# ConvNeXt block and two Mamba layers on one core: convolution bands read from DRAM in sliding runs, other group sizes, and a dt projection on three row groups

## The chip, the core and the metric

The kernel runs on one core of a Trainium2 chip. Times are microseconds of the device, from one launch of the whole program. The core has a matrix engine (PE, TensorE), a vector engine (DVE), an activation engine (ACT), a third engine for elementwise work and set-up (POOL, GpSimd), and SP, which here only issues transfers (DMA). Each engine works through its own list of instructions in order; a wait of one instruction holds all that stand behind it on that engine. SBUF is the on-chip memory with 128 partitions, PSUM the memory into which PE writes (8 banks of 128 x 512 floats), DRAM the memory outside.

## The reference

Input x is 32 x 96 x 56 x 56, float32. A ConvNeXt block comes first, then a Mamba block with two layers over the 3136 positions of each image, a fusion and a batch norm.

```python
# layer 0
h = depthwise_conv_7x7(x, conv_w, padding=3) + conv_b
h = layernorm over channels
h = gelu(h @ w1 + b1) @ w2 + b2          # 96 -> 384 -> 96
x1 = h * layer_scale + x
# layer 1, seq = x1 as (batch, 3136, 96)
for i in range(2):
    h = layernorm(seq); xs, z = split(h @ in_w)           # 192 each
    xc = silu(causal_conv4(xs) + conv_b)
    dt, Bm, Cm = split(xc @ xproj_w)                      # 6, 16, 16
    delta = softplus(dt @ dt_w + dt_b)                    # 192
    state = exp(delta * A) * state + delta * Bm * xc      # 192 x 16, a scan over positions
    seq = seq + ((state * Cm).sum + D * xc) * silu(z) @ out_w
out = fus_w @ concat(seq, relu(gp_w @ mean(x1))) + fus_b
out = batchnorm(out) + x1                                 # statistics over batch and positions
```

## The kernel before

**Groups of batches.** The depthwise convolution is done for two channels at a time (a pair; 48 pairs) as matmuls: the stationary operand is a band matrix that holds the seven vertical taps of one horizontal offset, the moving operand is the input with rows on partitions (112 = 2 x 56), batches and columns along the free dimension. Seven matmuls, one for each horizontal offset dw, add up in one PSUM bank. The batches come in groups (lines 101 to 103): the first has 12, then four of NB = 5. The output goes to DRAM (`conv_d`), 56 rows for each channel.

**Head.** `conv_pair` (line 158) does the first group for each pair: load x, write the seven vertical taps into three rotating band tiles with seven predicated copies on DVE (L165, masks made by POOL), store the band in DRAM (`band_d`), two halves of six batches with seven matmuls each (L176), an activation that adds the bias (L180), and the store (L184). Set-up of the weights stands between the third and the fourth pair in the program: POOL loads them, small matmuls (L270, L294, L301) fold norm and output weights. Then batch 0 goes through the rest of the ConvNeXt block.

**Loop.** 4 chunks of 784 positions for each of 32 images and 2 layers make 256 stages. A stage has 24 scans (slots), j = 0 to 5 for 32 channels each and g = 0 to 3 for four of the 16 states each. For each, ACT computes the exp (L904, after a copy of the carried state L903), DVE the product with B (`times_b`, L886) and the scan (L958), POOL the product with C (L963) and, for j = 2 and 5, that with B (`pooled`, L940); PE spreads u over the states (L930) and sums the result (L1004, `add_up`). Two exps and the spread values pass through the wide PSUM tiles. `gate` (L979) multiplies with silu(z).

All other work is put between the scans by an order written by hand. `put(m, pieces)` files each piece under a slot number of stage m (a fraction orders pieces in one slot), and the main loop emits, slot by slot, exps, `keep_state`, the scan, spreads, `add_up` and then the pieces. The numbers fix the order within each engine's list, not the time. Pieces of the stage are:

- `prep` of the next stage: norm, projections (L624), `dbl` and `dbl_out` (xproj, 38 output rows, L651 and L659), `dt` (L686: six matmuls of 6 rows by 64 columns, all from partitions 0 to 5), `softplus` (L694, three), `product` u = delta * xc on POOL (L706), and the loads that spread delta, B and C over partitions (`load_d4`, three buffers; `load_bc`; `store_u` and `load_u`).
- `post` of the stage before: output projection (`project`, L785 and L791) and `move` (L799 or L805), statistics.
- `block0`, the ConvNeXt block for half a chunk of a later image: centre (L371), squares (L376), norm, L443, gelu, L463, residual (L469).
- `conv`, one pair of a later group (192 of them, from stage 2 on): loads of band and x (`load`), seven matmuls (`tap`, L555), activation and store (`store`, L564, L567). All seven write PSUM bank set 2, which the third softplus has to release.

`keep_warm` (L916) issues spare matmuls into an unused part of a PSUM bank; `FILL` says how many go ahead of a spread. `KS` says how many scans after its own a state is kept, `AHEAD` where `pooled` stands.

**Tail.** Batch statistics, then for each half image two loads, an activation (L1108), an addition (L1109) and a store.

## Time and profile before

| | us |
|---|---|
| median of 3 runs | 15847.34 (15838.45 to 15850.79) |
| profiled execution, its time | 15850.69 |
| its span, first to last instruction | 15848.7 |
| first convolution on PE (L176) | 47.7 to about 446 |
| first to last scan (L958) | 565.3 to 15474.8 |

| instruction | mean ns | count |
|---|---|---|
| scan L958 | 1771 and 1776 | 6144 |
| product with B on DVE, L886 | 980 and 967 | 4096 |
| product with C on POOL, L963 | 3251 | 3072 |
| exp on ACT, L904 | 918 and 947 | 6144 |
| predicated copy L165 | 1038 | 336 |

A line of the profile names engine, source line, operation and tiles (out<-in). A matmul of float32 stands in the trace as two passes, each with a weight load of its own. "Idle before" is the time in which an engine stood still just before an instruction, with what released it. Busy time of instructions that follow each other directly overlaps a little, so that distances between starts are the better measure of pace.

### The profile page before, as it was taken

To read this page: it belongs to the slowest core of one execution; us is meant where nothing else is said; L and a number is where in the kernel's file an instruction comes from. 1 tells how busy PE (TensorE), PEld (TensorE's weight loads), DVE (VectorE), ACT (ScalarE), POOL (GpSimd) and SP (SyncE) were. 2 spreads that over 40 slices of the span, in tenths; PEclk is the share of its full clock that TensorE was granted. 3 is DMA by queue.
4 is the path that set the end of the run, shared out by engine and by line. 5 is a ranking of instruction groups with operands and counts; after the bars stand their busy time and mean duration, and the time that the engine had idled before them with its cause. 6 is when DMAs were issued, how large, how long until landed. Compare 5 with 4: busy or idle time off the path is not lost. (4 is left out here: it accounts for less than half of the span.)

```text
span 15848.7 us, 213573 instructions
## 1 busy us (share of the span) xinstructions
PE 13987.3 (88%) x74328; PEld 5953.8 (38%) x74328; DVE 15121.7 (95%) x11782; ACT 11958.4 (75%) x23139; POOL 14379.5 (91%) x4766
## 2 busy tenths in 40 slices
PE   8899999999999999999999999999998888888870
PEld 5333333333333333333333333333333333333320
DVE  8699999999999999999999999999999999999993
ACT  1587777778787787877777787877777777777763
POOL 1599999999999999999999999999999999999990
PEclk9899999999999999999999999999999999999985
DMA  4355545455545454545455455455444444444438
GB/s 111 110 149 150 154 148 153 148 150 153 152 148 153 148 151 151 152 148 152 149 150 154 147 153 149 150 151 152 148 151 136 140 142 137 137 138 143 138 126 293
DMA packets 1307217, 2362.54 MB, mean 149 GB/s; under 512 B 495918, under 2 KB 697914, under 8 KB 1306136
## 3 DMA queue, kind: packets, MB, share of 16 engines
q1 hardware_dynamic: 1296808, 2308.46, 48.1%
q10 hardware_dynamic: 7168, 38.54, 0.6%
q8 instruction: 585, 9.58, 0.2%
q14 instruction: 496, 4.06, 0.1%
q0 software_dynamic: 2160, 1.88, 0.1%
HBM read 1945.97 MB, written 402.41 MB: 148 GB/s over the span
## 5 line engine op out<-in xcount | busy, mean ns | idle before, releaser
L963 POOL TENSOR_TENSOR h<-h,cp 128x1568 f32<-128x1568 f32 x3072 | 9938.5, 3251 | 548.4 <-DVE h L958 467.0
L958 DVE TENSOR_TENSOR_SCAN h<-w,h 128x785 f32<-128x785 f32 (+1 forms) x3072 | 5299.7, 1771 | 117.2 <-ACT w L904 100.7
L958 DVE TENSOR_TENSOR_SCAN h<-da,w 128x785 f32<-128x785 f32 (+1 forms) x3072 | 5391.0, 1776 | 2.7 <-ACT da L904 2.7
L940 POOL TENSOR_TENSOR h<-us,bp 128x1570 f32<-128x1570 f32 x1024 | 3321.2, 3243 | 31.0 <-PE y L1004 19.3
L904 ACT ACTIVATE w<-d,A 128x784 f32<-128x784 f32 x3072 | 2819.0, 918 | 500.5 <-DVE h L958 419.0
L886 DVE TENSOR_TENSOR w<-w,bp 128x786 f32<-128x786 f32 x3072 | 2916.4, 980 | 200.1 <-PE w L930 85.4
L904 ACT ACTIVATE da<-d,A 128x784 f32<-128x784 f32 x3072 | 2876.7, 947 | 14.9 <-DMA d<-dd 14.1
L1004 PE MATMUL y<-h,ssum 128*32 128x392 f32 x24576 | 2590.9, 511 | 59.2 <-POOL h L963 59.2
L624 PE MATMUL ps<-hn,wx 97*64 97x392 f32 x12288 | 2202.8, 500 | 28.4 <-POOL hn L615 28.4
L930 PE MATMUL w<-u,sel 64*128 64x393 f32 x4096 | 986.4, 556 | 940.8 <-DVE h L958 929.3
L1004 PEld LDWEIGHTS y<-h,ssum 128*32 128x32 f32 x24576 | 691.0, 111 | 1710.8 <-issue 1356.4
L624 PEld LDWEIGHTS ps<-hn,wx 97*64 97x64 f32 x12288 | 812.2, 136 | 1353.2 <-issue 1285.3
L555 PE MATMUL ps<-xpad,band 112*112 112x280 f32 x2688 | 909.8, 458 | 284.0 <-ACT dl L694 284.0
L903 ACT COPY w<-st 128x1 f32<-128x1 f32 x2304 | 371.0, 161 | 1038.6 <-DVE h L958 1005.6
L916 PEld LDWEIGHTS y<-sel 128*128 128x128 f32 x7680 | 920.0, 192 | 251.2 <-DVE h L958 113.7
L886 DVE TENSOR_TENSOR h<-w,bp 128x786 f32<-128x786 f32 x1024 | 990.3, 967 | 0.5 <-DMA bp<-bd 0.5
L367 ACT ACT_TABLE_LOAD x759 | 973.8, 1283 | 14.2 <-PEq L1157 0.8
L916 PE MATMUL y<-sel 128*128 128x120 f32 x7680 | 967.5, 279 | 12.1 <-DVE z L979 12.1
L615 POOL TENSOR_TENSOR hn<-seq,hn 96x784 f32<-96x784 f32 x256 | 478.1, 1868 | 462.3 <-ACT hn L388 455.4
L791 PE MATMUL ps<-z,ow 64*96 64x392 f32 x3072 | 849.2, 706 | 0.0
L930 PEld LDWEIGHTS w<-u,sel 64*128 64x128 f32 x4096 | 329.5, 188 | 1328.2 <-DVE h L958 748.9
L555 PEld LDWEIGHTS ps<-xpad,band 112*112 112x112 f32 x2688 | 437.6, 186 | 868.0 <-ACT dl L694 402.6
(159 smaller groups left out, 16539.9 us busy)
## 6 DMA issues: line engine op xcount, KB each, us to landing
d<-dd SPq DMA_DIRECT2D x1536, 392.0 KB, 3.7
bp<-bd SPq DMA_DIRECT2D x1024, 392.0 KB, 5.5
cp<-bd SPq DMA_DIRECT2D x1024, 392.0 KB, 6.6
us<-uu SPq DMA_DIRECT2D x512, 392.0 KB, 5.0
dd<-dl SPq DMA_DIRECT2D x512, 294.0 KB, 3.8
band<-band_d SPq DMA_DIRECT2D x192, 343.0 KB, 7.8
uu<-u SPq DMA_DIRECT2D x1024, 49.0 KB, 2.6
cv<-conv_d SPq DMA_DIRECT2D x256, 147.0 KB, 2.7
```

The costliest lines, as they stand in the source:

```text
L367: nc.scalar.preload_act_table_set("natural_log_exp_and_others")
L555: nc.tensor.matmul(v["ps"][0:R2, 0 : NB * W], v["band"][:, dw, :], xpad[:, :, dw : dw + W], start=(dw == 0), stop=(dw == 6),)
L624: nc.tensor.matmul(v["x", q][rows(a), 0:HC], weights[:, k, 64 * q : 64 * q + 64], v["hn"][:, o : o + HC], start=(k == 0), stop=(k == last),)
L791: nc.tensor.matmul(v["ps"][a][0:C, 0:HC], S.d["ow"][rows(a), q, :], S.z[rows(a), q, :], start=False, stop=(q == NQ - 1),)
L886: nc.vector.tensor_tensor(halves(S.pb[j, g]), halves(S.u4[j])[:, :, 0 : HC + 1], halves(S.bc[0, g // 2][:, g % 2, :]), ALU.mult,)
L904: nc.scalar.activation(e[:, 1 : 1 + CH], S.d4[j], AF.Exp, scale=S.d["A"][:, j, g : g + 1])
L916: nc.tensor.matmul(spare, sel[:, 0, :], sel.rearrange("p a b -> p (a b)")[:, 0 : 512 - HC], start=True, stop=True,)
L930: nc.tensor.matmul(u4[:, 512 * a : 512 * a + HC + 1], sel[rows(a), j % 2, :], S.u[rows(a), j // 2, a : a + HC + 1], start=True, stop=True,)
L940: nc.gpsimd.tensor_tensor(states(S, j, h)[:, :, 0 : 1 + CH], S.us[j].unsqueeze(1).broadcast_to([128, 2, 1 + CH]), S.bc[0, h][:, :, 0 : 1 + ...
L958: nc.vector.tensor_tensor_scan(h[:, g % 2, at], S.e.pop((j, g))[:, at], S.pb.pop((j, g), h[:, g % 2, :])[:, at], 1.0 if c else 0.0, ALU.mu ...
L963: nc.gpsimd.tensor_tensor(h[:, :, 0:CH], h[:, :, 1 : 1 + CH], S.bc[1, g // 2], ALU.mult)
L1004: nc.tensor.matmul(S.y[r0 : r0 + 32, 0:HC], ssum, hs[k][:, g, tok(a)], start=False, stop=(half == 1 and g == 1),)
```

## The change

There are six parts.

1. Groups: 8 batches first, then four groups of 6.
2. Bands: one line of 1024 floats for each channel holds its taps at a pitch of 128, 14 copies of it are written to DRAM, and a band tile is loaded with two transfers in which each partition reads a run of 896 floats (3584 bytes) that starts one float earlier than that of the partition before. Masks, predicated copies and the store of bands go.
3. Output rows of a channel lie at a pitch of 64 in PSUM and in `conv_d`; 120 rows are computed and stored, eight of them unused.
4. xproj has 128 output rows; dt's six rows appear three times, at partitions 0, 32 and 64, B and C at 96 to 127. The tile shares the buffer of the gelu. The dt projection takes its three groups from these three places, the third first, and softplus follows that order.
5. FILL from 3 and 12 to 1 and 11, KS from 2 to 3, AHEAD exchanged for j = 2. `warm(0)` calls `keep_warm` with zero matmuls.
6. Slots of many pieces.

```diff
+HP = 64
+REP, PER = 14, 1024
-    NB = 5
+    NB = 6
-    groups = [(0, b0)] + [(b, b + NB) for b in range(b0, B, NB)]
+    groups = [(0, b0)] + [(b, min(b + NB, B)) for b in range(b0, B, NB)]
...
-    band_d = dram.tile([C // 2, 2 * H, 7 * 2 * H], F32, name="band_d")
+    band_d = dram.tile([C, REP * PER], F32, name="band_d")
...
+    cw = cc.tile([C, 49], F32, name="cw")
+    nc.sync.dma_start(cw, conv_w)
+    line = cc.tile([C, PER], F32, name="line")
+    nc.vector.memset(line, 0.0)
     for dh in range(7):
...
+        nc.vector.tensor_copy(
+            line.rearrange("p (k n) -> p k n", n=P2)[:, 0:7, HP + H + 2 - dh],
+            cw[:, 7 * dh : 7 * dh + 7],
         )
...
+    for lo in range(0, C, 24):
+        r = slice(lo, lo + 24)
+        nc.sync.dma_start(
+            band_d[r].rearrange("c (r n) -> c r n", n=PER),
+            line[r].unsqueeze(1).broadcast_to([24, REP, PER]),
         )
...
+    def load_band(T, p):
+        for j in range(2):
+            w = band_d[2 * p + j]
+            nc.sync.dma_start(
+                T[j * H : (j + 1) * H],
+                bass.AP(
+                    w.tensor, w.offset + HP + H - 1 - HP * j,
+                    [[PER - 8, H // 8], [PER - 1, 8], [1, 7 * P2]],
+                ),
+            )
...
-        for dh in range(7):
-            nc.vector.copy_predicated(
-                T,
-                masks[dh].unsqueeze(1).broadcast_to([R2, 7, R2]),
-                cw[:, p, dh * 7 : (dh + 1) * 7].unsqueeze(2).broadcast_to([R2, 7, R2]),
+        load_band(T, p)
+        ps = cps.tile([M2, b0 * W], F32, name="ps")
+        for dw in range(7):
+            nc.tensor.matmul(
+                ps, T[:, dw * P2 : dw * P2 + M2], xp[:, :, dw : dw + W],
+                start=(dw == 0), stop=(dw == 6),
             )
-        nc.sync.dma_start(band_d[p], T.rearrange("p k n -> p (k n)"))
...
+        ct = cx.tile([M2, b0 * W], F32, name="ct")
+        nc.scalar.activation(ct, ps, AF.Identity, bias=cb[0:M2, p : p + 1])
+        nc.sync.dma_start(conv_d[0][p * P2 : p * P2 + M2, :], ct)
...
+        d["xp"] = const.tile([128, NQ, 128], F32, name=f"xp{i}", tag=f"xp{i}")
+        nc.vector.memset(d["xp"], 0.0)
+        for q in range(NQ):
+            nc.vector.tensor_copy(d["xp"][:, :, 32 * q : 32 * q + DTR], xp[:, :, 0:DTR])
+        nc.vector.tensor_copy(d["xp"][:, :, 128 - 2 * NS :], xp[:, :, DTR:NX])
...
-                (-6, load), (2, load_x), (11.2, center), (11.9, square), (12.4, mean),
-                (12.6, root), ((14.1, norm) if ZP else (14.1, True, norm)), (15, up), (15.2, gelu), (17.3, down),
-                (17.7, residual),
+                (-6, load), (2, load_x), (11.2, center), (12.1, square), (12.4, mean),
+                (12.6, root), ((14.6, norm) if ZP else (14.6, True, norm)), (15, up), (15.2, gelu), (17.4, down),
+                (18.8, residual),
...
-            at = (5.7, 5.9, 8, 8.7, 9, 9.4, 10.2)
-            return [(-1, load), (10.3, store), *[(at[dw], tap(dw)) for dw in range(7)]]
+            at = (5.4, 6.5, 8, 8.7, 9, 9.4, 10.2)
+            return [(-0.5, load), (11.8, store), *[(at[dw], tap(dw)) for dw in range(7)]]
...
-        AHEAD = {(2, 0): 0.5, (2, 1): 4.4, (5, 0): 12.3, (5, 1): 16.9}
+        AHEAD = {(2, 0): 4.9, (2, 1): 0.8, (5, 0): 11.2, (5, 1): 16.9}
...
-                v["dbl"] = wp.tile([NX, CH], F32, name="dbl", tag="dbl", bufs=1)
+                t = wp.tile([128, NF, HC], F32, name="gl", tag="gl", bufs=1)
+                v["dbl"] = t.rearrange("p f n -> p (f n)")[:, 0:CH]
...
-                    for a in range(2):
+                for a in range(2):
+                    for q in (2, 0, 1):
+                        r = slice(32 * q, 32 * q + DTR)
                         nc.tensor.matmul(
-                            v["dt", q][rows(a), 0:HC], d["dtw"][:, 64 * q : 64 * q + 64],
-                            v["dbl"][0:DTR, tok(a)], start=True, stop=True,
+                            v["dt", q][rows(a), 0:HC], d["dtw"][r], v["dbl"][r, tok(a)],
+                            start=True, stop=True,
                         )
...
-                for q in range(NQ):
+                for q in (2, 0, 1):
                     nc.scalar.activation(
...
-                (-18, load), (-12.3, center), (-11.9, square), (-12.1, halo), (-11.6, mean),
-                (-11.2, root), (-9.5, norm),
+                (-18, load), (-12.2, center), (-11.9, square), (-17, halo), (-11.6, mean),
+                (-11.4, root), (-9.5, norm),
...
-            t = (-4.5, -4.4, -5.8, -4.8, -4.2, 0.2, 1.3, 2.3, 2.9, 3.4, 4)
+            t = (-4.5, -4.4, -5.8, -4.5, -4.2, -0.2, 1.3, 2.7, 2.9, 3.9, 5.1)
...
-                (max(10, t[8] + 1.2), load_bc(0, 0)), (max(10.2, t[8] + 1.2), load_bc(1, 0)),
-                (max(16.8, t[8] + 2.2), load_bc(1, 1)), (max(19.8, t[8] + 2.2), load_bc(0, 1)),
+                (max(10.1, t[8] + 1.2), load_bc(0, 0)), (max(10.2, t[8] + 1.2), load_bc(1, 0)),
+                (max(19.5, t[8] + 2.2), load_bc(1, 1)), (max(17.2, t[8] + 2.2), load_bc(0, 1)),
...
-                (max(14, t[10] + 1.5), product), (max(17.1, t[10] + 3.1), store_u(0)),
-                (29, store_u(1)),
-                (max(18.1, t[10] + 2), load_d4(0)), (max(21.9, t[10] + 3), load_d4(1)),
-                (max(20.3, t[10] + 3.2), load_u(0)), (24, load_d4(2)),
-                (26.9, load_d4(3)), (32.9, load_u(1)), (30, load_d4(4)), (34, load_d4(5)),
+                (max(16.7, t[10] + 1.5), product), (max(18.9, t[10] + 3.1), store_u(0)),
+                (27, store_u(1)),
+                (max(13.9, t[10] + 2), load_d4(0)), (max(21.9, t[10] + 3), load_d4(1)),
+                (max(22, t[10] + 3.2), load_u(0)), (24, load_d4(2)),
+                (27.1, load_d4(3)), (32.9, load_u(1)), (28.1, load_d4(4)), (30.2, load_d4(5)),
...
-            pieces = [(7.9, project), (8.9, move(0)), (9.2, move(1))]
+            pieces = [(7.5, project), (8.7, move(0)), (9.1, move(1))]
...
-                pieces += [(12.7, save), (17.2, stat(0)), (18.7, stat(1))]
+                pieces += [(12.7, save), (17.2, stat(0)), (20.9, stat(1))]
...
-        KS = 2
-        FILL = {0: 3, 4: 12}
+        KS = 3
+        FILL = {0: 1, 4: 11}
...
+            put(m, [(4.5, warm(0)), (12.5, warm(0))])
```

## The prediction

> **What bounds the kernel now.** First the page's busy times: four engines carry load, and VectorE (DVE) nearly all of the span.
>
> ```profile
> PE 13987.3 (88%) x74328; PEld 5953.8 (38%) x74328; DVE 15121.7 (95%) x11782; ACT 11958.4 (75%) x23139; POOL 14379.5 (91%) x4766
> ```
>
> A mean over stages hides where the rest is, so next the busy time by stretches (columns: stretch, length, then PE, weight loads, DVE, ACT, POOL, then granted PE clock, DMA share, GB/s): the first convolution, a piece of the scan loop with convolution in it, one without, and the last pass.
>
> ```profile
> 100.00:400.00 300.00, 300.00 (x1054) 184.00 (x1053) 273.54 (x264) 40.54 (x75) 0.00 (x0) 1.00 0.45 120
> 2700.00:4700.00 2000.00, 1846.42 (x9950) 785.93 (x9952) 1971.34 (x1522) 1592.66 (x3110) 1930.04 (x630) 0.95 0.50 151
> 13200.00:15200.00 2000.00, 1747.09 (x9368) 707.23 (x9362) 1954.10 (x1510) 1554.62 (x3031) 1915.40 (x625) 0.92 0.44 139
> 15440.00:15840.00 400.00, 27.53 (x144) 9.54 (x144) 153.19 (x105) 130.67 (x117) 36.65 (x12) 0.53 0.89 291
> ```
>
> Three regimes, then. The head (to the first scan, 565 us) is bound by PE: 300 of 300 us. The loop (256 stages of 24 scans, 565 to 15476, so 58.2 us each) is bound by DVE, 98.6% busy in one row and 97.7% in the other; the row with the lower clock is the one with less DVE work done. The tail (some 370 us of it) is bound by DMA, and the diff doesn't touch it.
>
> In the head the timeline gives the pace:
>
> ```profile
> 299.79 146.19 PE L176 MATMUL ps<-xpad,band 112*112 112x336 f32 x512
> 302.27 7.49 DVE L165 COPY_PREDICATED band<-mi,cw 112x784 f32<-112x784 int32 x7 [0.52 <-PE ps L176]
> 310.26 7.50 DVE L165 COPY_PREDICATED band<-mi,cw 112x784 f32<-112x784 int32 x7 [0.49 <-PE ps L176]
> ```
>
> 512 passes in 146.19 us are 0.2855 us each; a matmul is two passes, a pair of channels 14 matmuls, so 7.99 us, which is the distance of the two DVE rows (310.26 - 302.27). DVE needs 7.5 of it and waits for PE: PE sets the pace.
>
> In the loop the waits tell what could be won (waiter, line, releaser: total, times, longest):
>
> ```profile
> DVE h L958 <- ACT w L904: 100.7, 114, 2.6
> DVE w L886 <- PE w L930: 85.4, 83, 47.7
> ACT sq L564 <- PE ps L555: 327.1, 192, 2.9
> ACT seq L799 <- PE ps L791: 104.0, 74, 2.7
> ```
>
> DVE waits 100.7 us for exps and 37.7 for spreads (85.4 less the single wait of 47.7 before the loop runs), with small ones some 145 us. That is the ceiling of what reordering can win here. ACT's waits for PE precede them: ACT is in order, and an exp stands behind the activation that waits.
>
> **The change, head.** (1) Batches 12 to 8. A pair takes 7 matmuls of 8 x 56 = 448 columns instead of 14 of 336. In proportion to columns a pass is 0.2855 x 448/336 = 0.381 us, 14 passes 5.33 us. 48 pairs: 255.8 against 383.7, so -128 us. The output rows (120 for 112) don't lengthen a pass. ACT's copy, 0.54 us for 336 columns twice, is one of about 0.7: hidden under PE.
>
> (2) The band. The 336 predicated copies (1.04 us) and 21 selects go; one line per channel is made by 7 small copies and written 14 times to DRAM, 5.5 MB. At the 291 GB/s of the tail that is 19 us, behind the bias loads, whose issue took 2.1 and 10.2 us on SP; the first band can be in SBUF at some 45 to 50 us.
>
> (3) PE's order moves: the built program has all twelve set-up matmuls (norm weights, folded output weights) ahead of the first pair; before, one was ahead and the others lay between pairs.
>
> ```profile
> L301 PE MATMUL ps<-fw,owt x12: 246/297/422, 85.0 to 92.5; 96*64 96x96 f32 x12
> ```
>
> Their last ran at 92.5, but between convolution matmuls. Their inputs are POOL's small loads, issued until 70.6 us; the one that counts (ow of the second layer) was issued at 62.9-64.1 and takes 4.2 to land, then three rounds of some 1.5 us: about 73. The loads themselves meet 5.5 MB of band writes; POOL loses about 9 us of selects and clears. Bounds 65 and 90 us; I take 75, since the chain keeps its loads. So the convolution runs from 75 to 75 + 255.8 + 0.7 = 331.5 us instead of from 47.7 to 446.5: head -115 us (-125 to -100). Work after it (446.5 to 565) stays.
>
> (4) The pace needs the loads. A pair moved 952 KB in 7.99 us at 0.45 DMA share; now it moves 201 (x) + 401 (band) + 215 (store) = 817 KB in 5.33 us, which is 153 GB/s, share 0.58 by that row: hidden. [...] By the row the loads take 3.1 us of 5.33[...]
>
> **The change, loop.** (5) Convolution taps, 280 to 336 columns: by columns a pass goes from 0.238 (0.2855 x 280/336) to 0.2855 us, fourteen passes +0.67 us of PE in each of 192 stages. (6) The dt projection goes from one group of array rows to three, so that its six matmuls can stand side by side instead of two and two.
>
> ```profile
> 4078.76 2.56 PE L686 MATMUL ps<-dbl,dtw 6*64 6x392 f32 x12
> 4082.94 1.67 PE L555 MATMUL ps<-xpad,band 112*112 112x280 f32 x4 [1.62 <-ACT dl L694]
> 4084.40 2.74 PE L785 MATMUL ps<-seq,eye 96*96 96x392 f32 x4
> ```
>
> Before, 2.56 us for twelve passes in two column groups. Bounds: 2.56 (no gain) and two passes, 0.65; the nearest row is this pairing itself, so I take 1.2, -1.3 us. Three spare matmuls of 120 columns fewer per stage (FILL, 15 to 12; two passes of 0.10): -0.6. In sum PE has about 1.2 us less a stage; as PE doesn't bound, this pays only through what waits for it.
>
> (7) It does: the second row shows PE idle 1.62 us for the third softplus, which frees the bank of the taps. With group 2 first, tap 0 starts two activations (0.96 us) earlier; two longer taps cost 0.2 to 0.4 back, so the project behind (L785, L791), for which ACT's move waits, comes about 0.6 us earlier. A stall of that chain is 0.73 us long (DVE waits at 3511.9 for an exp that stood behind a move released at 3511.2). (8) The residual and the convolution's store go one exp later in ACT's queue, as do the squares. This removes stalls of the kind below, where DVE lost 2.59 us because the exp stood behind the residual:
>
> ```profile
> 12486.03 1.79 DVE L958 TENSOR_TENSOR_SCAN h<-w,h 128x785 f32<-128x785 f32 x1 [2.59 <-ACT w L904]
> 12484.32 0.58 ACT L469 ACTIVATE xin<-ps,b2ls 96x392 f32<-96x392 f32 x1 [2.85 <-PE ps L463]
> ```
>
> What is late next is the residual's own store, with a wait of half a stage before its reader. Between nothing and 145 us, I take 60 (four tenths; the chains of (7) and (8) are most of the 100.7, but not all of each goes).
>
> (9) Moves on SP and POOL. The product goes behind one more L963, yet POOL's row has the same sum, and its gap of 1.06 us a stage stays. On SP the fifth d4 load goes ahead of the store of delta and waits for an exp of scan 7: that store goes some 6 us later, about 15 us ahead of its reader. The sixth goes ahead of the u load of group 5 and waits for an exp of scan 11, at 4093.6; the u load then lands (median 5.0) near 4099, where POOL wanted it at 4099.2. The 1.06 us gap behind hides it; without it POOL, with only 1.6 us free in a stage, would be late. The keep_state and halo moves and warm(0), which issues nothing, cost nothing: 0.2 us copies beside ACT's 25% idle.
>
> [...] In the stage from 4069.4 PE's longest gap is 1.62 us, and yet the clock between 4083 and 4090 was 0.76. [...]by the row it may: kept as a rival.
>
> **Sum.** Against the profiled execution (span 15848.7, time 15850.69): head -115, loop -60, so 15675.7. The median of the runs is 3.35 below that execution: 15672, taken as 15670.
>
> **Rivals.** *Loop unchanged*: the DVE rows are 98% busy, and stalls can move instead of going. Then 15847 - 115 = 15732. *DMA bounds the pairs*: [...]against it the DMA share of 0.45. *All stalls go*: -115 - 140: 15592. *Slower*: PE's shorter dt and fewer fillers leave its clock halved for one more window of about 3.4 us in slots 4 to 9; PE is then 1.7 us late at the project, 0.6 of it already won, and DVE waits about 0.5 us in every stage. The row at clock 0.92 against 0.95 gives the sign: 17 us per 2000 us, 0.5 a stage. 256 x 0.5 = +128 against -115: 15860. It decides from 0.45 us a stage on, and ends slower from 0.57.
>
> **How the numbers follow.** Likeliest 0.50 (15620 to 15720 on its own), loop unchanged 0.20, DMA bound 0.12, all stalls gone 0.08, halved clock 0.10. A measurement tells 0.2%, 32 us, from no change. All but the last are faster; of the last half is slower, 0.04 the same. Range 15570 to 15790: it takes in the first four.
>
> **What would show it.** Right: L178 passes of some 0.38 us, pairs 5.3 us apart from 65-90 to about 330; the first scan near 450; L700's twelve passes in under 1.6 us; the exp waits of L972's scans under 60 us. Wrong: gaps of PE for band loads in the head; a granted clock under 0.93 in the loop with longer waits of the scan for exps; POOL waiting for us.

## The result

The changed kernel takes 15760.28 us (median of 4 runs, 15745.14 to 15764.96) against 15842.9 of the kernel before on the same chip: ratio 0.9946, 95% interval [0.9929, 0.9963]. That is 83 us less, 0.5%; 177 were forecast. The direction and the range were right, the size was off by a factor of two.

Where the time went, in the two profiled executions (first to last scan is the distance between the starts of the first and the last scan):

| stretch | before | after | difference | forecast |
|---|---|---|---|---|
| start to first scan | 565.3 | 466.4 | -98.9 | -115 |
| first to last scan | 14909.5 | 14924.0 | +14.5 | -60 |
| last scan to the end | 373.9 | 369.5 | -4.4 | 0 |
| span | 15848.7 | 15759.8 | -88.9 | -175 |

So the head gave most of what it should, and the loop gave nothing that can be told from noise (see the experiments). First the page's busy times of the changed kernel, then the stretches that answer to those of before (columns as there):

```profile
PE 13461.7 (85%) x72120; PEld 5646.6 (36%) x72120; DVE 14771.9 (94%) x11457; ACT 11966.7 (76%) x23091; POOL 14367.3 (91%) x4746
```

```profile
100.00:300.00 200.00, 200.00 (x528) 95.77 (x528) 0.00 (x0) 23.47 (x37) 0.00 (x0) 1.00 0.55 155
2600.00:4600.00 2000.00, 1798.16 (x9752) 762.75 (x9750) 1969.82 (x1523) 1596.21 (x3108) 1929.36 (x631) 0.95 0.51 153
13100.00:15100.00 2000.00, 1677.64 (x9182) 680.23 (x9174) 1952.53 (x1509) 1560.98 (x3030) 1914.56 (x624) 0.91 0.43 138
```

DVE's predicated copies in the head are gone (336 of 1.04 us), and it is idle there (0.00 of 200 us in the first row). In the loop it is as busy as before (1969.82 of 2000 against 1971.34), although PE is busy 48 us less in a stretch of the same length. Most of the gain sits in the first row: PE works without a gap. The timelines of the head give its pace, of PE and of ACT:

```profile
99.83 200.59 PE L178 MATMUL ps<-xpad,band 112*120 112x448 f32 x528
...
103.82 0.63 ACT L183 ACTIVATE ct<-ps,cb 120x448 f32<-120x448 f32 x1 [4.68 <-PE ps L178]
109.14 0.63 ACT L183 ACTIVATE ct<-ps,cb 120x448 f32<-120x448 f32 x1 [4.68 <-PE ps L178]
```

200.59 / 528 is 0.380 us a pass and 5.32 us lie between two pairs. In the loop the table of waits shows that those which were to go did shrink, and that one has grown, that of the gate (waiter, line, releaser: total, times, longest; the last line is the gate's of the kernel before):

```profile
DVE w L900 <- PE w L947: 93.8, 40, 49.1
DVE h L975 <- ACT w L918: 63.9, 80, 3.3
DVE z L996 <- PE y L1021: 63.9, 76, 6.1
...
ACT sq L575 <- PE ps L565: 159.4, 192, 2.5
...
ACT seq L813 <- PE ps L805: 54.0, 33, 2.7
...
DVE z L979 <- PE y L1004: 13.0, 5, 5.3
```

The scan's waits for an exp fell from 100.7 to 63.9 us, ACT's for the taps from 327.1 to 159.4, for the project from 104.0 to 54.0. Those for spreads, without the single one before the loop, rose from 37.7 to 44.7. Against that the gate (L996) now waits 63.9 us for the summed result; it was 13.0. By slots, over stages 4 to 249: DVE's waits before the scan of slot 10 fell from 54.7 to 21.8 us, those before the scan of slot 19 from 31.0 to nothing, and the gate, which stands between the scans of slots 19 and 20, got 46.5.

To compare loops I use one number per stage, its loss: the distances from the start of each scan to that of the next, less the undisturbed distance of the same slot (its 5th percentile), summed over the 24 slots. It is worked out from the starts of scans in the kept traces. Over the 184 stages 10 to 193, which have convolution taps, the mean is 0.62 us before and 0.64 after. The stalls moved; the sum stayed.

### The profile page after: what moved, and what is told of

Same layout as the page of the kernel before. It is cut to its first block, busy times and chain, and to the rows that moved or that the text cites. A ratio compares the mean times of both kernels' runs of the same rounds, so it can differ in the third digit from the quotient of the medians.

```text
span 15759.8 us, 207713 instructions
## 1 busy us (share of the span) xinstructions
PE 13461.7 (85%) x72120; PEld 5646.6 (36%) x72120; DVE 14771.9 (94%) x11457; ACT 11966.7 (76%) x23091; POOL 14367.3 (91%) x4746
## 5 line engine op out<-in xcount | busy, mean ns | idle before, releaser
L975 DVE TENSOR_TENSOR_SCAN h<-w,h 128x785 f32<-128x785 f32 (+1 forms) x3072 | 5287.1, 1769 | 73.0 <-ACT w L918 63.9
L565 PE MATMUL ps<-xpad,band 112*120 112x336 f32 x2688 | 1060.1, 512 | 331.4 <-ACT dl L708 331.4
L930 PEld LDWEIGHTS y<-sel 128*128 128x128 f32 x6144 | 747.1, 192 | 259.0 <-issue 97.0
L930 PE MATMUL y<-sel 128*128 128x120 f32 x6144 | 794.6, 279 | 21.1 <-DVE z L996 21.1
L384 ACT ACTIVATE sq<-ps 96x392 f32<-96x392 f32 x768 | 378.7, 493 | 557.6 <-PE ps L379 392.7
L565 PEld LDWEIGHTS ps<-xpad,band 112*120 112x120 f32 x2688 | 449.6, 191 | 935.2 <-ACT dl L708 446.5
```

The costliest lines, as they stand in the source:

```text
L565: nc.tensor.matmul(v["ps"][0:M2, 0 : nb * W], band[:, dw * P2 : dw * P2 + M2], xpad[:, 0:nb, dw : dw + W], start=(dw == 0), stop=(dw == 6),)
L930: nc.tensor.matmul(spare, sel[:, 0, :], sel.rearrange("p a b -> p (a b)")[:, 0 : 512 - HC], start=True, stop=True,)
L975: nc.vector.tensor_tensor_scan(h[:, g % 2, at], S.e.pop((j, g))[:, at], S.pb.pop((j, g), h[:, g % 2, :])[:, at], 1.0 if c else 0.0, ALU.mu ...
```

## The experiments

Medians are of 4 or 5 executions (21 for conv_only and softplus_order, 13 for after_taps280); ratios are to the kernel before (after: as above). "Loop" is first to last scan in the one profiled execution. Three executions with the very same loop code gave 14924.0, 14920.5 and 14912.8. A profiled execution can lie further off: that of fill_back took 16.5 us less than its kernel's median and that of loop_only 15.6 less, those of bias_row 14.5 and conv_dt 10.0 more. So a loop difference under some 15 us says nothing, and where these four stand in one the medians decide.

| run | what it is | median | ratio | first scan | loop |
|---|---|---|---|---|---|
| before | | 15841 to 15847 | 1 | 565.3 | 14909.5 |
| conv_only | before + convolution's part | 15822.7 | 0.9988 | 462.6 | 14988.4 |
| conv_dt | conv_only + dt, softplus order | 15797.5 | 0.9966 | 463.9 | 14962.7 |
| fill_back | the change with FILL of before | 15762.0 | 0.9945 | 467.3 | 14903.7 |
| after | the change | 15760.3 | 0.9946 | 466.4 | 14924.0 |
| taps280 | conv_only, shorter taps | 15738.4 | 0.9931 | 462.5 | 14902.5 |
| after_taps280 | the change, shorter taps | 15830.7 | 0.9992 | 468.5 | 14996.7 |
| loop_only | before + all but the convolution's part | 15931.6 | 1.0055 | 565.8 | 14980.4 |
| loop_fill | loop_only with FILL of before | 15914.1 | 1.0045 | 565.8 | 14981.2 |
| dt_before | before + dt, softplus order | 15925.2 | 1.0053 | 569.5 | 14982.3 |
| softplus_order | before + softplus order | 15858.8 | 1.0010 | 568.5 | 14921.9 |
| conv_dt_sq4 | conv_dt, four buffers for squares | 15763.8 | 0.9952 | 465.3 | 14923.8 |
| bias_row | the change, biases as one row | 15724.6 | 0.9926 | 439.2 | 14920.5 |

### What each part does to the loop

Four kernels stand between the two. The first takes only the convolution's part; the second adds the dt projection:

```diff
 # conv_only: the changed kernel, but
-            at = (5.4, 6.5, 8, 8.7, 9, 9.4, 10.2)
+            at = (5.7, 5.9, 8, 8.7, 9, 9.4, 10.2)
...
-        FILL = {0: 1, 4: 11}
+        FILL = {0: 3, 4: 12}
 # and all other slots, KS, AHEAD, xproj and dt as before
 # conv_dt: the same, but xproj, dt and the softplus order of the change
```

> The changed kernel with the loop's slots, FILL, KS, AHEAD, xproj and dt projection of the kernel before: only the groups, the sliding bands and the row pitch are new. Theory A (the loop's gain was given back by the matrix engine's clock, which fewer spare matmuls let fall): first scan near 466 us as in the changed kernel, first to last scan 14910 (+-10) as in the kernel before, so some 100 us faster than before in all (15745). Theory B (the larger taps, 336 columns for 280, cost the loop): first to last scan 14930 to 14960, and 40 to 80 us faster in all (15765 to 15800).

> As the run with the convolution's part alone, but with the dt projection on three row groups and the softplus order of the changed kernel; slots, FILL, KS and AHEAD as before. Theory A: the exps' waits in slot 10 fall by half (54.7 to some 25 us), first to last scan 14870 to 14900, time 15705 to 15735. Theory C (a stall removed from slot 10 comes back at the next meeting point, whatever the fillers): first to last scan within 10 us of the run with the convolution's part alone. The twelve passes of dt take 1.2 us or less against 2.56.

The convolution's part alone brings 18 us (ratio 0.9988 [0.9982, 0.9995]): 103 in the head, of which the loop takes 79 back. That was theory B, and more than the 20 to 50 us it allowed for the loop. The dt projection and softplus order take 26 off the loop and 25 off the time. That lies between the two theories of conv_dt: the waits of slot 10 did fall to 25 us as theory A had it, but the loop stayed far above its 14900. The slots with KS and AHEAD (from conv_dt to fill_back) take 36 off the time; the 59 between the two profiled loops are too large, since one execution was slower and the other faster than its median. FILL comes last:

```diff
 # fill_back: the changed kernel, but
-        FILL = {0: 1, 4: 11}
+        FILL = {0: 3, 4: 12}
```

> The changed kernel with 3 and 12 spare matmuls in place of 1 and 11. Theory A: the granted clock in slots 15 and 16 is full again (lost 0.44 us a stage now), the gate's waits for the summed result (L996 for L1021, 63.9 us) fall below 20, the loop is 30 to 60 us shorter: 15700 to 15730. Theory C: the gate's waits stay above 45 and the time is within 10 us of the changed kernel (15750 to 15770).

The clock in slots 15 and 16 came back to full and the gate's waits fell from 63.9 to 33.6 us, but the median is the same (15762.0 against 15760.3). Over the 184 stages the loss in slot 19 fell from 32 us to nothing, that in slots 12 to 14 rose from 21 to 53: a stall that moved. Theory A fell on it, since its lost clock was real and its return brought nothing; theory C's time (15750 to 15770) came true.

So in this order of steps a gain of the forecast size was there (25 and 36 us by the medians, in place of 60), but on a loop that the convolution's part had first made 79 us longer. The next run asks whether it is the length of the taps:

```diff
 # taps280: conv_only, but
-                        v["ps"][0:M2, 0 : nb * W], band[:, dw * P2 : dw * P2 + M2],
-                        xpad[:, 0:nb, dw : dw + W],
+                        v["ps"][0:M2, 0 : (5 if dw else nb) * W], band[:, dw * P2 : dw * P2 + M2],
+                        xpad[:, 0 : 5 if dw else nb, dw : dw + W],
```

> The run with the convolution's part alone, but in the loop only the first of the seven taps covers all six batches of a later group, the other six cover five (280 columns in place of 336): most of the convolution of the sixth batch of each later group is left out. Theory L (the 79 us that the convolution's part adds to the loop, 14988.4 us from first to last scan against 14909.5, come from the length of the taps): 14915 to 14930, time 15755 to 15775. Theory D (they come from the band in two transfers of runs, the stores with 120 rows, or the other row pitch): 14970 or more, time 15810 to 15830.

Theory L, and more than it asked (14915 to 14930): some 0.57 us less of PE's work a stage (by columns, twelve passes of 280 in place of 336) takes 86 us off the loop, and 84 off the time. Band loads in two transfers, stores of 120 rows and the pitch cost nothing that shows: the loop takes 14902.5 us with them and 14909.5 in the kernel before.

### The loop's part by itself

```diff
 # loop_only: the kernel before with dt, softplus order, slots, FILL, KS, AHEAD of the change
 # dt_before: the kernel before with dt and softplus order only
 # softplus_order: the kernel before, but
-                for q in range(NQ):
+                for q in (2, 0, 1):
```

> The kernel before with only the loop's part of the change that is not convolution: dt on three row groups, softplus order, slots, FILL, KS, AHEAD. Theory P (steps 6 to 8 were right in their place, and the convolution's longer taps took their gain): first to last scan 14830 to 14860 in place of 14909.5, time 15765 to 15795. Theory C (stalls removed come back at the next meeting point by themselves): 14890 or more, 15825 or more. With the taps short, the gate's waits for the summed result stay under 25 us by theory P, over 45 by theory C.

> The kernel before with only dt on three row groups and the softplus order. Theory P (steps 6 and 7 right in their place): the exps' waits of slot 10 (54.7 us) fall by half or more, first to last scan 14909.5 to 14870-14890, time 15800 to 15820. Theory C (a stall that goes comes back at the next meeting point): 14900 to 14920, 15830 to 15850. Theory K (1.3 us less of PE's work lets its clock fall and costs more than it brings): 14930 or more, 15860 or more.

> The run with the loop's part alone on the kernel before (15931.6), with 3 and 12 spare matmuls as before in place of 1 and 11. Theory A (fewer spare matmuls let PE's clock fall in slots 15 and 16, and the summed result comes late to the gate): clock lost there 0.53 us a stage to under 0.1, the gate's waits 72.5 us to under 25, first to last scan 14980.4 to 14930 or less, time 15885 or less. Theory C (the gate's waits go and others take their place): 14965 or more, 15915 or more.

> The kernel before with only the softplus order of the change (third group first). Theory P (step 7: tap 0 comes 0.96 us earlier, and so the project and its move): waits of slot 10 from 54.7 to 25-40 us, first to last scan 14880 to 14900. Theory K (what comes earlier before the spread of slot 10 widens the gap there, clock lost in slots 11 and 12 from 0.03 to 0.4-0.8 a stage): 14915 to 14950, time 15850 to 15885; the rest of the 73 us belongs to the shorter dt.

This was the surprise. On the kernel before, the loop's part makes it slower: ratio 1.0055 [1.0041, 1.0069]. The dt projection with its softplus order alone does the same, 1.0053 [1.0041, 1.0066]; putting the spare matmuls back in loop_fill leaves the profiled loop where it was (14981.2 against 14980.4) and the medians 17.5 us apart, with intervals that overlap (ratio 1.0045 against 1.0055), so their share is small at most. The softplus order alone costs 12 us of the loop and 15 of the time, with 0.65 us of lost clock a stage in slots 11 and 12, as theory K had it. So theory P fell. Theory C, for which stalls only come back, left loop_only open (14890 or more), but not dt_before (14900 to 14920). K was right in size: a dt projection that is 1.6 us shorter, with its softplus order, made the loop 73 us longer. (The edit also widens xproj to 128 rows and lets its result share the gelu's buffer. Neither shows in the trace: the copy of that result takes 476 ns in both kernels, and PE's weight loads wait 179 us for it in place of 197.) Each half of the change alone costs the loop 71 or 79 us, both together 14.5.

The trace of dt_before shows how. Its PE around slot 10 (start, duration; idle before in brackets):

```profile
4106.97 0.97 PE L697 MATMUL ps<-gl,dtw 6*64 6x392 f32 x12
...
4118.74 1.21 PE L563 MATMUL ps<-xpad,band 112*112 112x280 f32 x4
4122.33 1.68 PE L941 MATMUL w<-u,sel 64*128 64x393 f32 x4 [2.38 <-DVE h L969]
4123.94 1.27 PE L563 MATMUL ps<-xpad,band 112*112 112x280 f32 x2
```

and the kernel before at the same place:

```profile
4092.48 1.21 PE L555 MATMUL ps<-xpad,band 112*112 112x280 f32 x4
4094.22 0.93 PE L930 MATMUL w<-u,sel 64*128 64x393 f32 x4 [0.54 <-DVE h L958]
4095.08 0.73 PE L555 MATMUL ps<-xpad,band 112*112 112x280 f32 x2
```

dt takes 0.97 us in place of 2.56, the taps that follow are done sooner, and the spread, which has to wait for a scan, now stands behind a gap of 2.38 us in place of 0.54. After the gap the same four passes take 1.68 us in place of 0.93. The stretches of dt_before say why (columns as above; the PE clock is the third number from the end):

```profile
4119.50:4122.50 3.00, 0.62 (x4) 0.17 (x4) 3.00 (x3) 2.90 (x7) 2.82 (x2) 0.95 0.00 1
4122.50:4126.00 3.50, 3.50 (x14) 1.18 (x18) 3.40 (x4) 0.95 (x4) 3.36 (x2) 0.50 0.84 220
4126.00:4130.00 4.00, 4.00 (x21) 1.36 (x10) 3.56 (x4) 1.37 (x6) 4.00 (x2) 0.62 0.89 340
```

PE's clock is halved after the gap (the record of it starts at 4122.2), and PE is busy all of the next row. The centring (L379) and the squares come late, then the exps, then DVE, in ACT's and DVE's rows:

```profile
4129.39 0.49 ACT L384 ACTIVATE sq<-ps 96x392 f32<-96x392 f32 x1 [2.63 <-PE ps L379]
```

```profile
4135.90 1.79 DVE L969 TENSOR_TENSOR_SCAN h<-w,h 128x785 f32<-128x785 f32 x1 [0.80 <-ACT w L915]
```

The trace's clock records come in pieces of 3.41 us (here 6.83 us at half). At half clock, half of a piece is lost, 1.71 us. Sorting the 184 stages by what they lost so in slots 10 to 12 (under 0.3 us, up to 1.9, more) gives nearly the same price in five kernels:

| kernel | stages with no / one / two half-clock pieces | loss in slots 11 to 15, us a stage, each |
|---|---|---|
| before | 181 / 3 / 0 | 0.08 / 0.66 / - |
| softplus_order | 124 / 50 / 10 | 0.09 / 0.67 / 2.26 |
| dt_before | 56 / 105 / 23 | 0.13 / 0.72 / 2.27 |
| after_taps280 | 73 / 93 / 18 | 0.14 / 0.68 / 2.19 |
| after | 173 / 2 / 9 | 0.13 / 0.80 / 2.10 |

With a fourth buffer for the squares it is lower (row_fill_sq4, below: 0.15, 0.40 and 1.72). Over the whole stage one piece is no worse than none (0.79 us in dt_before, against 0.84): the stages without a piece lose 0.61 between the scans of slots 9 and 10, those with a piece next to nothing there. A stage with two loses 2.40. Against the mean of 0.62 before, that is some 12 us from the 56 stages without a piece, 18 from the 105 with one and 41 from the 23 with two: more than half of what dt_before adds comes from one stage in eight.

### Both ways tested: shorter taps in the changed kernel

```diff
 # after_taps280: the changed kernel with the edit of taps280
```

> The changed kernel, but six of the seven taps of the later groups cover five batches in place of six (280 columns for 336; most of the convolution of the sixth batch of each later group is left out). Theory K (the longer taps fill the gap that the shorter dt leaves; too short is as bad as too long): with 0.57 us less of PE's work a stage the loop gets longer, 14924 to 14960 or more, time 15795 or more. Theory L (taps cost by their length, as in the old order, where the same cut took 86 us off): 14840 to 14890, time 15680 to 15730.

The same edit that took 86 us off the old order's loop adds 73 to the changed one's (15830.7 us, ratio 0.9992 [0.9983, 1.0]). The scan's waits for exps more than double:

```profile
DVE h L975 <- ACT w L918: 154.1, 192, 3.3
```

The clock is lost again in slots 10 to 12, in 111 of the 184 stages against 11 with the long taps. The two parts of the change thus need each other: the longer taps fill the hole that the short dt leaves, and the short dt makes room for them.

### Filling the gap with spare matmuls

```diff
 # dt_bridge: dt_before, and at slot 9.5 eight spare matmuls in the project's bank
+        def bridge():
+            ps = psum(0)
+            for _ in range(8):
+                nc.tensor.matmul(ps[:, 0 : 512 - HC], sel[:, 0, :], ..., start=True, stop=True)
 # dt_zeros4, dt_zeros8: the same with zeros, added to the convolution's own sum
+                    nc.tensor.matmul(v["ps"][0:R2, 0 : 512 - HC], v["band"][:, 0, :], zeros,
+                        start=False, stop=False)
```

> The run with the dt projection and softplus order on the kernel before (15925.2, first to last scan 14982.3), with eight spare matmuls more in each stage with convolution, in the bank of the finished projection, between the sixth tap and the spread of slot 10, where PE stood still for 1.22 us in slot 10 (2.4 us in one stage looked at). Theory K (this gap lets the clock fall to half for 3.4 us in slots 11 and 12, 1.42 us lost a stage, and squares, exps and scans of slots 12 to 15 come late): clock lost there under 0.4, first to last scan 14930 or less though PE does 1.8 us more of work a stage, time 15875 or less. Theory O (the order of dt and softplus itself is late for ACT, the clock only follows): 14965 or more, 15905 or more.

> The run with the dt projection and softplus order on the kernel before (15925.2; first to last scan 14982.3), with four matmuls of zeros (120 columns, some 0.9 us in all at full clock) added to the convolution's sum in each stage with convolution, between the sixth tap and the spread of slot 10. They wait for nothing that the taps don't wait for, unlike the spare matmuls of the run before, which stood for a move of ACT. PE's gap there is mostly 1.7 to 2.4 us long. Theory K: the gap falls to some 1.1 us, the clock lost in slots 11 and 12 from 1.42 us a stage to under 0.7, first to last scan 14950 or less, 15895 or less, though PE has more to do. Theory O (dt's order itself makes ACT late, the clock follows): 14975 or more, 15915 or more.

> As the run with four, with eight (some 1.8 us at full clock), which fill the gap. Theory K: clock lost in slots 11 and 12 under 0.3, first to last scan 14900 to 14940, 15845 to 15885; where the eight reach into the spread of slot 10, some of it is given back. Theory O: 14975 or more, more than with four.

All three took the lost clock of slots 11 and 12 from 1.40 us a stage to 0.0, and all three were far slower: 16392.9, 16166.6 and 16384.7 us. They ran into another limit, which ACT's waits name, of the run with eight zeros first, then of that with four (433.2 us in 180 waits in dt_bridge, none in dt_before):

```profile
ACT sq L384 <- DMA conv_d<-sq: 421.0, 181, 5.2
...
ACT sq L384 <- DMA conv_d<-sq: 253.1, 96, 4.3
```

The squares share three buffers with the convolution's store. When the last taps end later, the store is issued later, and the third square has to wait until that transfer gives its buffer back; PE then stands still for the square (slot 13, 1.57 us a stage with eight zeros), and norm and exps follow. So the time of these runs doesn't tell what the lost clock costs: what removed it brought something worse.

The trace of dt_zeros4 does tell, stage by stage. All of its 96 waits for the buffer lie in stages of even number; in the odd ones the zeros take the lost clock away and no such wait comes (us a stage, 92 even and 92 odd stages of the 184):

| kernel | clock lost in slots 10 to 12, even / odd | loss in slots 11 to 15, even / odd | loss of the stage, even / odd |
|---|---|---|---|
| before | 0.04 / 0.02 | 0.16 / 0.03 | 0.81 / 0.42 |
| dt_before | 1.22 / 1.58 | 0.66 / 0.80 | 1.10 / 0.91 |
| dt_zeros4 | 0.00 / 0.00 | 2.94 / 0.12 | 3.55 / 0.74 |

In odd stages dt_before loses 0.77 us more in slots 11 to 15 than the kernel before; with the clock kept up, and the dt projection and softplus order as they are, 0.68 of it is gone. Theory O, in which dt's order makes ACT late and the clock only follows, does not fit that. What the whole stage wins is less, since 0.50 us now lie in slot 2 (0.10 before), in exp waits that come after a late even stage; they were not traced further. Zeros together with a fourth buffer would show whether the time comes back too; that was not tried.

### The limit on the late side

conv_only has the same wait, where its longer taps end late (waits of ACT, then its timeline in one such stage):

```profile
ACT sq L376 <- DMA conv_d<-sq: 47.4, 24, 2.8
```

```profile
3902.85 0.54 ACT L567 ACTIVATE sq<-ps,cb 120x336 f32<-120x336 f32 x1 [2.91 <-PE ps L557]
...
3908.54 0.49 ACT L376 ACTIVATE sq<-ps 96x392 f32<-96x392 f32 x1 [1.60 <-DMA conv_d<-sq]
```

24 waits are one in every eighth stage, where the pool and fuse matmuls of a finished image stand among the taps and PE is latest: these stages take 60.87 us in place of 58.77. A fourth buffer removes the wait (run on conv_dt, where it was 52.0 us):

```diff
-            sq = work([P2, HC], "sq", 3)[0:C]
+            sq = work([P2, HC], "sq", 4)[0:C]
```

> The run with the convolution's part and the dt projection, old slots, but with four buffers in place of three for the squares, which the convolution's store shares. Theory Q (in one stage of eight the longer taps push the convolution's store so late that the third square waits for the store's transfer to give its buffer back, 24 waits of together 52.0 us on ACT, and DVE waits behind): these waits are gone, first to last scan 14962.7 to some 14915, time 15797 to 15750. Theory B (PE's backlog from the longer taps itself, not the buffer): 14945 or more, 15780 or more.

Theory Q, a little short: the waits are gone, the loop is 39 us shorter, the time 34. If it is worth as much in conv_only, where it was not run, about half of what the longer taps cost in the old order was this buffer. The rest would be PE's backlog before the spread of slot 10 (loss in slot 11: 44 us in conv_only, 13 before). In the changed kernel no such wait is in the table: its third square waits 0.82 us for the first one's mean instead.

### The head

```diff
 # bias_row: the changed kernel, but
-        nc.sync.dma_start(
-            cb[j * HP : j * HP + H].unsqueeze(2), bv[j].partition_broadcast(H)
-        )
+    nc.sync.dma_start(cbr, conv_b.rearrange("c one -> one c").partition_broadcast(P2))
...
+        nc.vector.tensor_copy(cb[r], cbr.rearrange("p (k two) -> p two k", two=2)[r, j, :])
```

> The changed kernel, with the convolution's biases loaded as one row of 96 floats to 128 partitions and spread by two copies on VectorE, in place of two loads of 2688 single floats each. Theory H1 (SyncE spends 14.6 us to issue these loads, and their 5376 elements stand before POOL's small loads): the band lines go out some 15 us earlier, POOL's last weight load for the folded output weights is issued at some 65 in place of 81, the convolution starts near 72 in place of 90, first scan near 448 in place of 466: 15740 or some 18 us less. Theory H2 (POOL's loads are slow by themselves, eight at a time, each with its own latency): start and first scan within 4 us of the changed kernel.

SP, POOL and PE in the head of the changed kernel, from their timelines (transfers: start, time to issue; then as above):

```profile
2.02 14.58 SPq L144 DMA_DIRECT2D cb<-in_conv_b  x2
16.65 19.36 SPq L171 DMA_DIRECT2D xpad<-in_x  x1
36.06 8.77 SPq L137 DMA_DIRECT2D band_d<-line  x4
...
18.28 0.54 POOL L245 DMA_DIRECT2D w_sb<-in_w  x1 [11.26 <-DMA g<-in_ln_g]
...
85.86 0.55 PE L299 MATMUL ps<-ident,ow 64*96 64x64 f32 x2 [2.52 <-DMA ow<-in_out_w]
...
90.06 15.24 PE L178 MATMUL ps<-xpad,band 112*120 112x448 f32 x32
```

and of bias_row:

```profile
1.65 1.03 SPq L170 DMA_DIRECT2D xpad<-in_x  x2
3.49 7.14 SPq L137 DMA_DIRECT2D band_d<-line  x4
...
61.37 68.85 PE L177 MATMUL ps<-xpad,band 112*120 112x448 f32 x176
```

Two loads of 2688 single floats held SP's queue for 14.58 us and the x load behind them for 19.36, so that the band lines went out at 36 us; POOL's first small load (issued at 2.24) landed only at some 18 us, and POOL, with eight loads issued, waited 11.26 us for it. With the row, the x loads issue in 1.03 us, the band lines go out at 3.49, POOL issues the last fold's weights at 53.8 in place of 80.5, the convolution starts at 61.37 in place of 90.06, and the first scan at 439.2 in place of 466.4: theory H1, with more than it promised. The time is 15724.6 us, ratio 0.9926 [0.9913, 0.9938], 36 us below the changed kernel; the intervals of the two overlap, but the two kernels below with the same row and loop came out alike (0.9925 and 0.9929).

```diff
 # pairs_first: bias_row, PE and ACT in the program's order in the head, six pairs before the set-up
-    for p in range(3):
-        conv_pair(p)
+    with tc.manual_schedule(engines={ET0.PE, ET0.Activation}):
+        for p in range(6):
+            conv_pair(p)
 # head_best: pairs_first with three buffers for the raw weights
```

> The run with the biases as a row, with PE and ACT in the program's order in the head: six pairs of the first convolution, then the twelve set-up matmuls, then the other 42. Theory S (only PE's order holds the first pair until the folded weights are there, 61.4 us): the first pair starts at some 35 us, when its band is in SBUF, first scan 439 - 26 = 413, time about 15700. Theory W (the first six pairs fetch bands and x against POOL's loads, and the set-up then waits between pairs): half of it or less, first scan 426 or later, time 15712 or more.

> The run with six pairs ahead of the set-up matmuls (first pair at 47.6 us, but then 11.5 us between pairs for the set-up, since the second layer's weights wait for one of two buffers), with three buffers for these weights. Theory S: the set-up takes some 5 us between the pairs, first scan 438 to 431, time some 7 us less (15716). Theory W (something else late there): 436 or more.

Theory W in pairs_first, in whose timelines of PE and POOL one reads

```profile
47.60 35.27 PE L177 MATMUL ps<-xpad,band 112*120 112x448 f32 x84 [47.60 <-DMA band<-band_d]
...
88.36 1.57 PE L271 MATMUL ps<-raw,m 96*97 96x384 f32 x2 [4.21 <-DMA raw<-in_in_w]
...
94.22 26.20 PE L177 MATMUL ps<-xpad,band 112*120 112x448 f32 x63
...
83.81 0.54 POOL L266 DMA_DIRECT2D raw<-in_in_w  x1 [21.36 <-PE ps L271]
```

The first pair starts at 47.6, when its band lands, but the set-up then takes 11.5 us between pairs, partly since POOL's load of the second layer's weights waited for a buffer. First scan 438.0 (15723.1 us). A third buffer takes 1.4 us off that stretch and brings the first scan to 435.1, between the two theories; the median, 15730.2, shows nothing of it.

### Two attempts on the loop

warm_gaps puts spare matmuls into PE's gaps of bias_row, row_fill_sq4 joins the pieces that seemed to help:

```diff
 # warm_gaps: bias_row, FILL of before, and
-            put(m, [(4.5, warm(0)), (12.5, warm(0))])
+            put(m, [(4, warm(5)), (8.5, warm(12 if m >= 194 else 0))])
 # row_fill_sq4: bias_row, FILL of before, four buffers for the squares
```

> The run with the biases as a row, with spare matmuls of 3 and 12 as before and more of them where PE stands still: five in slot 4 of every stage, twelve in slot 8 of the stages without convolution. Theory A (PE's lower clock after its gaps makes the waits of the loop): the clock lost in slots 4 to 8 falls from 2.2 us a stage to under 1.2, the loop gets 40 to 80 us shorter than 14920, time 15645 to 15685. Theory N (lower clock costs little, or the spare matmuls stand in the way of the taps): 15710 or more.

> The changed kernel with the biases as a row, 3 and 12 spare matmuls, and four buffers for the squares: the pieces that the runs point to, together. By theory Q the third square no longer waits 0.82 us in each stage for a buffer (158 us on ACT over the loop), the norm comes earlier, slots 13 to 15 lose 20 to 40 us of waits: first to last scan 14880 to 14900, time 15690 to 15710. By theory C: 14900 to 14920, 15710 to 15730.

warm_gaps raised the granted clock of the whole run from 0.927 to 0.945 and won nothing: loop 14926.1, 15749.8 us, slower than without (15739.9 to 15785.6 us against 15709.4 to 15739.1). The clock lost in slots 4 to 8 fell from 2.2 to 1.5 us a stage, not to the 1.2 expected. Why it got slower was not traced; the spare matmuls stand in front of the taps in PE's list. row_fill_sq4 took away the 158 us that ACT waited for the third square's buffer, and DVE's loop did not change (14925.3; 15738.2 us). It ended above theory C's range too (15710 to 15730). Theories A and Q fall for the changed kernel; what bounds its stages, 0.64 us above the undisturbed distance, these two did not reach.

## Why the forecast was right and wrong

The step that failed is the loop's sum: two changes of PE's work were added to "about 1.2 us less a stage" and priced at nothing, while the runs show that each of the two alone costs the loop 73 to 79 us, and that the 60 us of removed stalls were no net gain (+14.5 measured). The head's start is a smaller miss beside it (16 us). By steps:

(1) Right: 0.380 us a pass, with 120 output rows (0.381 by the columns alone), 5.32 a pair (5.33).

(2) and (3) Off by 15 us: the convolution started at 90.06, at the late bound of 90, not at 75, and the head's gain of 98.9 fell just outside its range of 100 to 125. The step that failed is "the chain keeps its loads". I had priced the bias loads by their old issue times, 2.1 and 10.2 us; they take 14.58 together, which is little more. But I gave nothing to what stands behind them: the x load took 19.36, the band lines went out at 36, and POOL's weights for the last fold were issued at 80.5, not at 62.9. bias_row takes the two loads away and the start comes 28.7 us earlier. Whether they held POOL's loads directly or through the late band lines, it doesn't separate.

(4) Right: the loads did not set the pace. The share is 0.55 (0.58 by the row), PE has no gap in 200 us. The rival in which DMA bounds the pairs, given 0.12, was an estimate of mine that nothing here shows.

(5) Wrong, and with (6) the main error: "as PE doesn't bound, this pays only through what waits for it", which let 0.67 us of taps a stage pass for nothing. taps280 measures the term: 86 us in the old order (and after_taps280: the same cut costs 73 in the new one, so that the term has no fixed price). I had judged PE's slack by the stage (88% busy). Of 4.6 us of idle time a stage before the change, slots 2 to 4 hold 2.6, slots 14 and 15 1.0, slots 22 and 23 0.6; slots 5 to 13, where taps, project and the spread of slot 10 stand, hold 0.45. There PE is as full as DVE.

(6) The size was right (0.97 to 1.27 us against 1.2; by columns, 0.2855 x 392/336 each, twelve passes one after another would be 4.0 us, so they do stand side by side), its worth was not: less work for PE was counted as harmless or good. Alone it costs some 60 us (73 with the softplus order, of which that order is 12), because it opens a gap after which the clock is halved (0.50 after 2.38 us in dt_before); the odd stages of dt_zeros4 show the link.

(7) and (8) The stalls named did shrink or go (slot 10 by 60%, the exps of slot 19 wholly; all exp waits to 63.9 us, just above the 60 set as a sign of being right), and the slots were worth 36 us in their place. What failed is the sum: four tenths of 145 us were taken as a net gain from counting stalls, with no look at whether the next meeting point would be free. In slot 19 it was not, as the gate's 46.5 us show; fill_back moves that stall once more at the same time.

(9) Nearly right: POOL now does wait for the u load, which was named as a sign of being wrong, but by little: 22.6 us in 52 waits (6.2 in 2 before), 0.9 at most, less than its gap of 1.06. That the gap hides all of it is likely and not shown by itself.

Rivals: the nearest was "loop unchanged" (15732); with the head's 16 us and the loop's 14.5 on top it is 15762. The slower one, PE's half clock from a shorter dt and fewer spare matmuls, was right as a mechanism and wrong in place and in company: in slots 11 and 12 rather than 4 to 9, at 0.39 us a stage in dt_before (1.01 against 0.62), and the longer taps cancelled nearly all of it. That the time still ended inside the range is partly luck: the range was wide enough for a loop that gained nothing. On the clock, the row that this rival rested on was borne out: 0.76 over the 7 us from 4083 to 4090, just after PE's gap of 1.62 us, is 3.4 us at half, and in dt_before the clock was 0.50 after a gap of 2.38 us.

## What to carry to other kernels

An engine's slack is to be read between the points where others wait for it, not over the stage: here PE had 8% idle and almost none where it counted. Work on such a stretch can be too short as well as too long, so two edits that move it must be priced together, and a forecast from the sum of removed stalls should assume that a stall moves unless the next wait of each has been looked up. In a set-up, count the elements of a load, not its bytes: here 21 KB in 5376 single floats cost 27 us (first scan at 466.4 us, with one row at 439.2).

## What was not expected of the hardware

In dt_before every one of the 128 stages (of 184) with a half clock in slots 10 to 12 has a pause of PE of 1.60 to 2.39 us around slot 10, and no other stage has one over 1.56; the half clock lasts 3.41 or 6.83 us. The length is no sharp limit: in the changed kernel some pauses of 2.18 us left the clock full. Three spare matmuls a stage (FILL 3 and 12 for 1 and 11) decided in slots 15 and 16 of the changed kernel between 0.44 us of lost clock a stage and none, and that made no difference to the time; with four buffers for the squares (row_fill_sq4) 0.39 stayed lost in spite of them. Loads of single floats held a whole queue: SP issued nothing else for 14.58 us.
